# Moving expert, softmax and scan-state work between engines in a one-core AdaLN block

## The chip, the core and the metric

The kernel runs on one core of a Trainium2 chip, in fp32. The metric is the device time of one execution in microseconds (us). The engines are called by the profile's names: PE is TensorE, DVE is VectorE, ACT is ScalarE, POOL is GpSimd, SP is SyncE; PEld is the load of weights into TensorE.

## What is computed

The input x is [8 sequences, 512 steps, 128 features]. Six modulation rows per sequence (sa, ca, ga, sb, cb, gb) are made from c. Then come a recurrent attention part and a mixture of 8 experts, each behind a layernorm with modulation. Cut to what matters:

```python
h = layernorm(x) * (1 + ca) + sa
# attention part: 8 heads, state of 16, so 128 softmaxes of 17 per token
hr = rmsnorm(h) * norm_w
v = hr @ W_v.T                                  # [B, T, 8, 16]
gates = softmax((hr @ W_a.T).reshape(B, T, 8, 16, 17))
a0, A = gates[..., 0], gates[..., 1:]
state[t] = einsum('bhij,bhj->bhi', A[t], state[t-1]) + a0[t] * v[t]   # scan over 512 steps
x = x + ga * (h + state.reshape(B, T, 128) @ W_out.T)
# experts: top 4 of 8, softmax over the chosen
h = layernorm(x) * (1 + cb) + sb
combine = softmax of the 4 largest of (h @ router.T + bias), 0 elsewhere
gate, up = split(h @ gate_up.T + bias)          # 256 each, per expert
gate = minimum(gate, 7); up = clip(up, -7, 7)
act = (up + 1) * gate * sigmoid(1.702 * gate)
y = sum over experts of combine * (act @ down.T + down_bias)
x = x + gb * y
```

## The kernel before

The 4096 tokens are cut into 32 tiles of 128 tokens: 16 time steps of all 8 sequences. Four tiles make a superchunk of 512 tokens; there are 8. Up to the scan a tile has its tokens on the partitions; the scan has 64 partitions, one for each pair of head and sequence; the experts have features on the partitions and 512 tokens along the line.

The work consists of these parts, written as Python generators:

- ln1 (L188): layernorm (L162 to L179, with two full-width products with modulation rows at L178 and L179) and the rms factor of a superchunk.
- gates (L203 to L248), for a tile: transpose (L209), five matmuls into PSUM chunks of 27, 27, 26, 26 and 22 softmax groups (L220), with v in the last. For each chunk DVE takes the maximum (L224) and subtracts it (L226), ACT raises it (L229). Then, over all 128 groups of 17 (2176 elements a partition), DVE sums (L234), takes the reciprocal (L235), multiplies (L238), and multiplies the a0 column by v (L241). Eight DMAs on SP's queue (L243), one for each head, turn the tile ee (tokens on partitions) into g (heads and sequences on partitions).
- scan (L250 to L262), 16 steps for a tile: a product of the 16x16 gates with the state before (L256) and a sum over 17 (L259), which writes the new state into ys in SBUF. Each step needs the one before.
- attn_out (L264 to L282): eight DMAs on SP turn ys back into yt (L269), then transpose (L273), copy (L275), the output matmul (L277), and the addition into r (L281).
- attn_post (L284 to L357), for a superchunk: residual (L287, L288), second layernorm, transposes to h2T (L293, L295), the router matmul pr (L300), ranking and softmax on small tiles (L305 to L340), which give comb, the weight of each expert for each token. Then comb is transposed (L345) and multiplied with the experts' output biases (L350); the result is where the sum y begins (L355).
- experts (L359 to L423), for two experts at a time: for each of two halves of 128 features, gate and up matmuls of 512 tokens (L365, L367); ACT adds biases (L371, L373) and takes the sigmoid (L375); DVE clips up (L382), multiplies by min(gate, 7) (L383) and by the sigmoid (L384). The down projection (L391) has act as the weights, 128 tokens at a time, so an expert takes eight matmuls of 128 columns, and its output pd has tokens on the partitions. The combination (L399) is four operations an expert, each with a weight per partition: y = pd * comb + y.
- finish (L425 to L432): product with gb (L427), residual (L428), four output DMAs on SP (L431).

The order comes from two places. In the main loop (L443 to L462), beside the 16 scan steps of tile c, the kernel writes out the other parts: attn_out of tile c-1, ln1, the gates of tile c+2, attn_post of the superchunk before (beside the first tile of a superchunk), and its experts, two beside each of the four tiles, then finish. After each scan step two pieces of this list are taken:

```python
        for _ in scan(c):
            next(other, None)
            next(other, None)
        run(other)
```

The Tile framework then orders the instructions of each engine when the kernel is built, by its own planning, and puts in the waits on semaphores; at run time every engine works through its own list in that order. In the built kernel all eight experts of a superchunk lie in one stretch. Pools limit how far parts run ahead: two buffers of ee, three of g and ys, and in PSUM two banks for gate chunks, three for gate and up, one for pd, and two for all the small ones (misc).

Of the kernel before, what the change touches and what calls it, by code (L numbers as in the profile page):

```python
# [9 lines left out]
F32 = mybir.dt.float32  # L10
# [9 lines left out]
SIG_MAX = 1.0 / (1.0 + math.exp(-ALPHA * LIMIT))  # L20
# [8 lines left out]
def adaln_block_kernel(  # L29
    ctx: ExitStack,  # L30
    tc: tile.TileContext,
    x: bass.AP,        # [B, T, D]
    norm_w: bass.AP,   # [D, 1]
    wa_t: bass.AP,     # [D, H*M*(M+1)]
    wv_t: bass.AP,     # [D, D]
    wo_t: bass.AP,     # [D, D]
    rw_t: bass.AP,     # [D, E]
    r_bias: bass.AP,   # [1, E]
    gu_t: bass.AP,     # [D, E*2I]
    gu_bias: bass.AP,  # [128, E*4]  # L40
    dn_t: bass.AP,     # [E, I, D]
    dn_bias: bass.AP,  # [E, D]
    c_in: bass.AP,     # [B, D]
    w_mod: bass.AP,    # [D, 6*D]
    out: bass.AP,      # [B, T, D]
# [4 lines left out]
    J = M + 1               # softmax width  # L50
    NG = H * M              # softmax groups per token
    TT = P // B             # time steps in a tile of 128 tokens
    NT = T // TT            # tiles
    KT = 4                  # tiles in a superchunk
# [5 lines left out]
    # (first softmax group, groups) of each PSUM bank; v goes into the last bank  # L60
# [12 lines left out]
    ps_misc = ctx.enter_context(tc.tile_pool(name="ps_misc", bufs=2, space=PS))  # L73
# [45 lines left out]
    # lower[e, f] = 1 where f < e: among equal logits the lower index goes first  # L119
# [6 lines left out]
    # up's bias with the 1 of (up + 1)  # L126
# [54 lines left out]
    # the parts below are generators: they yield where other work may come between  # L181
    h_tiles = {}      # superchunk -> (h, rms factor)
    g_tiles = {}      # tile -> gates for the scan
    y_tiles = {}      # tile -> scan states
    r_tiles = {}      # superchunk -> h + attention
    f_tiles = {}      # superchunk -> what the experts need
# [16 lines left out]
    def gates(c):  # L203
# [12 lines left out]
        for g0, n in CHUNKS:  # L216
            last = g0 + n == NG
            w = n * J + (D if last else 0)
            pg = ps_gate.tile([P, 512], F32, tag="pg", name=f"pg{c}_{g0}")
            nc.tensor.matmul(  # L220
                pg[:, :w], hnT, wav[:, g0 * J : g0 * J + w], start=True, stop=True
            )
            pg3 = pg[:, : n * J].rearrange("p (g j) -> p g j", j=J)
            nc.vector.tensor_reduce(mx[:, g0 : g0 + n], pg3, AX.X, ALU.max)  # L224
            e3 = ee[:, g0 : g0 + n, :]
            nc.vector.tensor_tensor(  # L226
                e3, pg3, mx[:, g0 : g0 + n].unsqueeze(2).to_broadcast([P, n, J]), ALU.subtract
            )
            nc.scalar.activation(e3, e3, AF.Exp)  # L229
            if last:  # L230
                nc.scalar.copy(v, pg[:, n * J : w])
            yield
        z = tile_p.tile([P, NG], F32, tag="z", name=f"z{c}")
# [4 lines left out]
        nc.vector.tensor_tensor(  # L238
            ee, ee, z.unsqueeze(2).to_broadcast([P, NG, J]), ALU.mult
        )  # L240
        nc.vector.tensor_tensor(ee[:, :, 0], ee[:, :, 0], v, ALU.mult)  # L241
# [8 lines left out]
    def scan(c):  # L250
        g = g_tiles.pop(c)
        ys = scan_p.tile([H * B, TT, M], F32, tag="ys", name=f"ys{c}")
        prev = state0 if c == 0 else y_tiles[c - 1][:, TT - 1, :]
# [8 lines left out]
        y_tiles[c] = ys  # L262
# [21 lines left out]
    def attn_post(s):  # L284
        r = r_tiles.pop(s)
        x1 = sc_p.tile([P, KT, D], F32, tag="x1", name=f"x1_{s}")
        nc.vector.tensor_tensor(r, r, mod_row(2), ALU.mult)  # L287
        nc.vector.tensor_tensor(x1, r, x_sb[:, s * KT : (s + 1) * KT, :], ALU.add)  # L288
        h2 = sc_p.tile([P, KT, D], F32, tag="h2", name=f"h2_{s}")
# [7 lines left out]
        # router: top 4 of 8, softmax over the chosen  # L297
# [44 lines left out]
        # the experts' output biases, weighted  # L342
# [5 lines left out]
        pb = misc_psum(f"pb{s}")  # L348
        for k in range(KT):
            nc.tensor.matmul(  # L350
                pb[:, k * D : (k + 1) * D], cT[:, k * P : (k + 1) * P], dnb_sb,
                start=True, stop=True,
            )
        y = sc_p.tile([P, KT, D], F32, tag="y", name=f"y{s}")
        nc.scalar.copy(y.rearrange("p k d -> p (k d)"), pb)  # L355
        f_tiles[s] = (x1, h2T, comb, y)
        yield  # L357

    def experts(s, es):  # L359
        x1, h2T, comb, y = f_tiles[s]  # L360
        acts = {}

        def front(e, ic):
# [6 lines left out]
            gt = ffn_p.tile([P, NW], F32, tag="gate", name=f"gate{s}_{e}_{ic}")  # L370
            nc.scalar.activation(gt, pgt, AF.Identity, bias=gub_sb[:, e, ic : ic + 1])  # L371
            up = ffn_p.tile([P, NW], F32, tag="up", name=f"up{s}_{e}_{ic}")
            nc.scalar.activation(up, pup, AF.Identity, bias=ub1_sb[:, e, ic : ic + 1])  # L373
            sg = ffn_p.tile([P, NW], F32, tag="sg", name=f"sg{s}_{e}_{ic}")
            nc.scalar.activation(sg, gt, AF.Sigmoid, scale=ALPHA)  # L375
            return gt, up, sg

        def back(e, ic, gt, up, sg):
            if ic == 0:
                acts[e] = ffn_p.tile([P, IC, NW], F32, tag="act", name=f"act{s}_{e}", bufs=2)  # L380
            # clip(up, -7, 7) + 1, min(gate, 7), sigmoid(1.702 min(gate, 7))
            nc.vector.tensor_scalar(up, up, 1.0 - LIMIT, 1.0 + LIMIT, ALU.max, ALU.min)  # L382
            nc.vector.scalar_tensor_tensor(up, gt, LIMIT, up, ALU.min, ALU.mult)  # L383
            nc.vector.scalar_tensor_tensor(acts[e][:, ic, :], sg, SIG_MAX, up, ALU.min, ALU.mult)  # L384

        def down(e):
            act = acts.pop(e)
            pd = ps_dn.tile([P, KT, D], F32, tag="pd", name=f"pd{s}_{e}")
            for k in range(KT):
                for ic in range(IC):  # L390
                    nc.tensor.matmul(  # L391
                        pd[:, k, :], act[:, ic, k * P : (k + 1) * P], dn_sb[:, e * IC + ic, :],
                        start=(ic == 0), stop=(ic == IC - 1),
                    )
            return pd

        def combine(e, pd):
            for k in range(KT):
                nc.vector.scalar_tensor_tensor(  # L399
                    y[:, k, :], pd[:, k, :], comb[:, k, e : e + 1], y[:, k, :], ALU.mult, ALU.add  # L400
                )
# [23 lines left out]
    def finish(s):  # L425
        x1, _, _, y = f_tiles.pop(s)
        nc.vector.tensor_tensor(y, y, mod_row(5), ALU.mult)  # L427
        nc.vector.tensor_tensor(y, y, x1, ALU.add)  # L428
        for k in range(KT):
            c = s * KT + k  # L430
            nc.sync.dma_start(out[:, c * TT : (c + 1) * TT, :], y[:, k, :])  # L431
        yield  # L432
# [5 lines left out]
    # ---- the pipeline: beside the scan of tile c run the gates of tile c + 2,  # L438
    # the output of tile c - 1 and a part of the experts of the superchunk before
# [67 lines left out]
```

## Time and profile before

Three runs: 1391.12 us median (1390.35 to 1391.66). The profiled execution has a span of 1390.6 us.

| what | us |
|---|---|
| median of the runs | 1391.12 |
| span of the profiled execution, its own time | 1390.6 |
| DVE busy | 1151.2 |
| PE busy | 675.7 |
| PE weight loads | 348.3 |
| ACT busy | 462.8 |
| POOL busy | 1.1 |
| DVE, clip of up (L382), 128 instructions of 423 ns | 54.2 |
| DVE, reciprocal of the sums (L235), 32 of 938 ns | 30.0 |
| DVE, a0 times v (L241), 32 of 374 ns | 12.0 |
| ACT, sigmoid (L375), 128 of 629 ns | 80.5 |
| ACT, exp of chunks (L229), 160 of 564 ns on average | 89.1 |

Busy times of the engines overlap, so they don't add up to the span. In a line of the profile's groups, the source line and engine come first, then the operation, the tile written and the tiles read with their shapes, the number of instructions, the busy time in us with the mean of one in ns, and last the time for which the engine was idle just before, with what ended most of that. The slices cut the span into 40 parts of 34.8 us; each digit is a busy share in tenths. The chain of work is followed back from the last instruction, from each step to what released it.

### The profile page before, as it was taken

How to read it: one execution, taken by the hardware profiler on the slowest of the kernel's cores; microseconds unless marked ns; L12 is line 12 of the kernel's file. 1: busy time of each engine (PE TensorE's matmuls, PEld its weight loads, DVE VectorE, ACT ScalarE, POOL GpSimd, SP SyncE). 2: the span in 40 equal slices, each digit the busy share in tenths (PEclk: the TensorE clock that was granted, in tenths of full speed). 3: DMA queues.
4: the chain of work that ended last, by engine and by line, in shares of the span. 5: the costliest groups of instructions: out<-in, count | busy, mean ns of one | idle time of the engine just before them, and what ended most of it. 6: DMA issues, size and time to landing. Idle time of an engine off the chain costs nothing.

```text
span 1390.6 us, 9491 instructions
## 1 busy us (share of the span) xinstructions
PE 675.7 (49%) x2181; PEld 348.3 (25%) x2181; DVE 1151.2 (83%) x2533; ACT 462.8 (33%) x850; POOL 1.1 (0%) x10
## 2 busy tenths in 40 slices
PE   1415049531594237830496315942369414771077
PEld 0101015310262014510153102620135201440044
DVE  3889699996999799996989969897898978888366
ACT  2401037320382115610373203821146102541054
POOL 0000000000000000000000000000000000000000
PEclk9755568865697667965688656976569756795579
DMA  6251514024330325005140242303241041501200
GB/s 199 32 60 14 60 21 49 1 32 45 36 31 10 44 25 65 2 11 63 20 51 0 30 48 33 34 10 38 31 50 17 10 54 20 61 1 21 24 0 8
DMA packets 80248, 47.39 MB, mean 34 GB/s; under 512 B 38064, under 2 KB 79296, under 8 KB 79936
## 3 DMA queue, kind: packets, MB, share of 16 engines
q1 hardware_dynamic: 78640, 42.03, 25.8%
q10 hardware_dynamic: 1552, 4.75, 1.0%
q14 instruction: 38, 0.31, 0.1%
q8 instruction: 18, 0.29, 0.1%
HBM read 6.91 MB, written 2.10 MB: 6 GB/s over the span
## 4 chain that ended last, share of the span: by engine, by line
DVE 40%; PE 32%; DMA 21%; issue 2%; SPq 2%; ACT 2%; DVEq 0%; ACTq 0%
DMA g<-ee 15%; PE pgt L365 9%; PE pd L391 8%; DVE g L256 8%; PE pup L367 8%; DVE ys L259 7%; DVE mx L224 5%; DVE z L234 5%; DMA yt<-ys 4%; PE pg L220 4%; DVE ee L226 4%; DVE ee L238 3%; SPq L243 2%; DVE z L235 2%; DMA x_sb<-in_x_dram 1%
## 5 line engine op out<-in xcount | busy, mean ns | idle before, releaser
L256 DVE TENSOR_TENSOR g<-g,ys 64x256 f32<-64x256 f32 x511 | 211.2, 413 | 107.0 <-DMA g<-ee 60.1
L220 PE MATMUL pg<-wav,hnT 128*128 128x459 f32 (+2 forms) x320 | 221.6, 815 | 133.5 <-DVE ee L226 108.7
L259 DVE TENSOR_REDUCE ys<-g 64x16 f32<-64x272 f32 x512 | 217.1, 424 | 11.3
L273 PE MATMUL py<-ident,yt 128*128 128x128 f32 x32 | 13.7, 427 | 436.5 <-DMA yt<-ys 435.8
L275 ACT COPY ytT<-py 128x128 f32<-128x128 f32 x32 | 8.5, 266 | 513.1 <-PE py L273 513.1
L391 PE MATMUL pd<-dn_sb,act 128*128 128x128 f32 x1024 | 146.6, 291 | 29.8 <-DVE act L384 16.2
L391 PEld LDWEIGHTS pd<-dn_sb,act 128*128 128x128 f32 x1024 | 136.2, 201 | 91.3 <-DVE act L384 36.6
L229 ACT ACTIVATE ee<-ee 128x459 f32<-128x459 f32 (+2 forms) x160 | 89.1, 564 | 201.4 <-DVE ee L226 179.6
L365 PE MATMUL pgt<-h2T,gu_sb 128*128 128x512 f32 x256 | 145.9, 654 | 0.0
L367 PE MATMUL pup<-h2T,gu_sb 128*128 128x512 f32 x256 | 138.8, 625 | 0.0
L220 PEld LDWEIGHTS pg<-wav,hnT 128*128 128x128 f32 x320 | 68.9, 254 | 257.2 <-issue 163.1
L273 PEld LDWEIGHTS py<-ident,yt 128*128 128x128 f32 x32 | 6.2, 193 | 461.3 <-issue 302.2
L224 DVE TENSOR_REDUCE mx<-pg 128x27 f32<-128x459 f32 (+2 forms) x160 | 95.1, 594 | 13.5 <-PE pg L220 12.8
L373 ACT ACTIVATE up<-pup,ub_sb 128x512 f32<-128x512 f32 x128 | 86.8, 678 | 40.8 <-PE pup L367 40.8
L371 ACT ACTIVATE gate<-pgt,gub_sb 128x512 f32<-128x512 f32 x128 | 87.6, 684 | 24.7 <-PE pgt L365 24.2
L226 DVE TENSOR_TENSOR ee<-pg,mx 128x459 f32<-128x459 f32 (+2 forms) x160 | 95.2, 595 | 0.0
L384 DVE SCALAR_TENSOR_TENSOR act<-sg,up 128x512 f32<-128x512 f32 x128 | 88.1, 688 | 7.4 <-ACT sg L375 3.4
L383 DVE SCALAR_TENSOR_TENSOR up<-gate,up 128x512 f32<-128x512 f32 x128 | 88.0, 688 | 2.9
L399 DVE SCALAR_TENSOR_TENSOR y<-pd,comb,y 128x128 f32<-128x128 f32 x256 | 74.9, 342 | 14.2 <-PE pd L391 13.9
L375 ACT ACTIVATE sg<-gate 128x512 f32<-128x512 f32 x128 | 80.5, 629 | 2.5
L234 DVE TENSOR_REDUCE z<-ee 128x128 f32<-128x2176 f32 x32 | 76.8, 2400 | 0.5 <-ACT ee L229 0.5
L238 DVE TENSOR_TENSOR ee<-ee,z 128x2176 f32<-128x2176 f32 x32 | 76.9, 2404 | 0.0
(89 smaller groups left out, 599.1 us busy)
## 6 DMA issues: line engine op xcount, KB each, us to landing
g<-ee SPq DMA_DIRECT2D x256, 136.0 KB
yt<-ys SPq DMA_DIRECT2D x256, 8.0 KB
x_sb<-in_x_dram SPq DMA_DIRECT2D x32, 64.0 KB
gu_sb<-in_gu_t_dram ACTq DMA_DIRECT2D x1, 2048.0 KB
out_dram<-y SPq DMA_DIRECT2D x32, 64.0 KB
wav<-in_wa_t_dram ACTq DMA_DIRECT2D x1, 1088.0 KB
wmod_sb<-in_w_mod_dram ACTq DMA_DIRECT2D x1, 384.0 KB
wo_sb<-in_wo_t_dram SPq DMA_DIRECT2D x1, 64.0 KB
```

Source lines behind the costliest of these rows:

```text
L220: nc.tensor.matmul(pg[:, :w], hnT, wav[:, g0 * J : g0 * J + w], start=True, stop=True)
L224: nc.vector.tensor_reduce(mx[:, g0 : g0 + n], pg3, AX.X, ALU.max)
L226: nc.vector.tensor_tensor(e3, pg3, mx[:, g0 : g0 + n].unsqueeze(2).to_broadcast([P, n, J]), ALU.subtract)
L229: nc.scalar.activation(e3, e3, AF.Exp)
L234: nc.vector.tensor_reduce(z, ee, AX.X, ALU.add)
L238: nc.vector.tensor_tensor(ee, ee, z.unsqueeze(2).to_broadcast([P, NG, J]), ALU.mult)
L256: nc.vector.tensor_tensor(a, a, prev.unsqueeze(1).to_broadcast([H * B, M, M]), ALU.mult)
L259: nc.vector.tensor_reduce(ys[:, t, :], g[:, t, :, :], AX.X, ALU.add)
L365: nc.tensor.matmul(pgt, gu_sb[:, e, ic * P : (ic + 1) * P], h2T, start=True, stop=True)
L367: nc.tensor.matmul(pup, gu_sb[:, e, I + ic * P : I + (ic + 1) * P], h2T, start=True, stop=True)
L384: nc.vector.scalar_tensor_tensor(acts[e][:, ic, :], sg, SIG_MAX, up, ALU.min, ALU.mult)
L391: nc.tensor.matmul(pd[:, k, :], act[:, ic, k * P : (k + 1) * P], dn_sb[:, e * IC + ic, :], start=(ic == 0), stop=(ic == IC - 1),)
```

## The change

- Gates: ACT copies the five PSUM chunks to ee. One DVE maximum over all 128 groups follows, then POOL subtracts it (2176 elements), one ACT exp covers the whole tile, DVE sums and takes the reciprocal, and POOL does the product with it and the product of the a0 column with v. The DMAs of g follow as before.
- Scan: the states are written into one PSUM bank yp with two halves, one for each parity of the tile, and the next step reads them from there. ACT copies a tile's states into ys in SBUF when its 16 steps are done; the yt DMAs read that.
- Experts: silu(1.702 gate + bias) on ACT takes the place of the identity and the sigmoid; the factor 1/1.702 goes into the weights of the combination. POOL clips up. One DVE operation, min with silu's value at 7 and product, takes the place of two. The down projection has the projection as weights and 512 tokens moving, so an expert takes two matmuls of 512 columns, and pd has features on the partitions.
- Combination: since tokens now lie along the line, weights must stand on all partitions. comb's transpose, over 1.702, is written to DRAM (cD) and read back with every partition getting all 8 x 512 values (wB, 2048 KB), both on ACT's DMA queue. DVE multiplies pd by wB's part, POOL adds to the sum yT.
- finish: eight matmuls transpose yT with the identity and add the weighted output biases, both into one bank; DVE reads that.
- Pools: misc has one PSUM bank instead of two (the states take the other), up five buffers, h2, y, yT and wB one each; x1 uses r's memory.

The core of the diff:

```diff
@@ gates
-            nc.vector.tensor_reduce(mx[:, g0 : g0 + n], pg3, AX.X, ALU.max)
-            e3 = ee[:, g0 : g0 + n, :]
-            nc.vector.tensor_tensor(
-                e3, pg3, mx[:, g0 : g0 + n].unsqueeze(2).to_broadcast([P, n, J]), ALU.subtract
-            )
-            nc.scalar.activation(e3, e3, AF.Exp)
+            nc.scalar.copy(ee[:, g0 : g0 + n, :], pg3)
...
+        nc.vector.tensor_reduce(mx, ee, AX.X, ALU.max)
+        yield
+        nc.gpsimd.tensor_tensor(
+            ee, ee, mx.unsqueeze(2).to_broadcast([P, NG, J]), ALU.subtract
+        )
+        yield
+        nc.scalar.activation(ee, ee, AF.Exp)
+        yield
...
-        nc.vector.tensor_tensor(
+        nc.gpsimd.tensor_tensor(
             ee, ee, z.unsqueeze(2).to_broadcast([P, NG, J]), ALU.mult
         )
-        nc.vector.tensor_tensor(ee[:, :, 0], ee[:, :, 0], v, ALU.mult)
+        nc.gpsimd.tensor_tensor(ee[:, :, 0], ee[:, :, 0], v, ALU.mult)
@@ scan
-        ys = scan_p.tile([H * B, TT, M], F32, tag="ys", name=f"ys{c}")
-        prev = state0 if c == 0 else y_tiles[c - 1][:, TT - 1, :]
+        ys = yp[:, c % 2, :, :]
+        prev = state0 if c == 0 else yp[:, (c - 1) % 2, TT - 1, :]
...
-        y_tiles[c] = ys
+        y_tiles[c] = scan_p.tile([H * B, TT, M], F32, tag="ys", name=f"ys{c}")
+        nc.scalar.copy(y_tiles[c], ys)
@@ attn_post
-        pb = misc_psum(f"pb{s}")
-        for k in range(KT):
-            nc.tensor.matmul(
-                pb[:, k * D : (k + 1) * D], cT[:, k * P : (k + 1) * P], dnb_sb,
-                start=True, stop=True,
-            )
-        y = sc_p.tile([P, KT, D], F32, tag="y", name=f"y{s}")
-        nc.scalar.copy(y.rearrange("p k d -> p (k d)"), pb)
-        f_tiles[s] = (x1, h2T, comb, y)
+        cA = ffn_p.tile([P, NW], F32, tag="w", name=f"cA{s}", bufs=2)
+        nc.scalar.mul(cA[:E, :], pc[:E, :], 1.0 / ALPHA)
+        cD = dram.tile([E, NW], F32, tag="cD", name=f"cD{s}")
+        nc.scalar.dma_start(cD, cA[:E, :])
+        wB = sc_p.tile([P, E, NW], F32, tag="wB", name=f"wB{s}", bufs=1)
+        nc.scalar.dma_start(wB, cD.rearrange("e n -> (e n)").unsqueeze(0).to_broadcast([P, E * NW]))
+        f_tiles[s] = (x1, h2T, cT, wB)
@@ experts
-            gt = ffn_p.tile([P, NW], F32, tag="gate", name=f"gate{s}_{e}_{ic}")
-            nc.scalar.activation(gt, pgt, AF.Identity, bias=gub_sb[:, e, ic : ic + 1])
-            up = ffn_p.tile([P, NW], F32, tag="up", name=f"up{s}_{e}_{ic}")
+            sg = ffn_p.tile([P, NW], F32, tag="sg", name=f"sg{s}_{e}_{ic}")
+            nc.scalar.activation(sg, pgt, AF.Silu, bias=gb_sb[:, e, ic : ic + 1], scale=ALPHA)
+            up = ffn_p.tile([P, NW], F32, tag="up", name=f"up{s}_{e}_{ic}", bufs=5)
             nc.scalar.activation(up, pup, AF.Identity, bias=ub1_sb[:, e, ic : ic + 1])
-            sg = ffn_p.tile([P, NW], F32, tag="sg", name=f"sg{s}_{e}_{ic}")
-            nc.scalar.activation(sg, gt, AF.Sigmoid, scale=ALPHA)
+            nc.gpsimd.tensor_scalar(up, up, 1.0 + LIMIT, 1.0 - LIMIT, ALU.min, ALU.max)
...
-            nc.vector.tensor_scalar(up, up, 1.0 - LIMIT, 1.0 + LIMIT, ALU.max, ALU.min)
-            nc.vector.scalar_tensor_tensor(up, gt, LIMIT, up, ALU.min, ALU.mult)
-            nc.vector.scalar_tensor_tensor(acts[e][:, ic, :], sg, SIG_MAX, up, ALU.min, ALU.mult)
+            nc.vector.scalar_tensor_tensor(up, sg, SILU_MAX, up, ALU.min, ALU.mult)
...
-            for k in range(KT):
-                for ic in range(IC):
-                    nc.tensor.matmul(
-                        pd[:, k, :], act[:, ic, k * P : (k + 1) * P], dn_sb[:, e * IC + ic, :],
-                        start=(ic == 0), stop=(ic == IC - 1),
-                    )
+            for ic in range(IC):
+                nc.tensor.matmul(
+                    pd, dn_sb[:, e * IC + ic, :], act[ic],
+                    start=(ic == 0), stop=(ic == IC - 1),
+                )
...
-            for k in range(KT):
-                nc.vector.scalar_tensor_tensor(
-                    y[:, k, :], pd[:, k, :], comb[:, k, e : e + 1], y[:, k, :], ALU.mult, ALU.add
-                )
+            if e == 0:
+                yT_tiles[s] = sc_p.tile([P, NW], F32, tag="yT", name=f"yT{s}", bufs=1)
+                nc.vector.tensor_tensor(yT_tiles[s], pd, wB[:, e, :], ALU.mult)
+                return
+            w = ffn_p.tile([P, NW], F32, tag="w", name=f"w{s}_{e}", bufs=2)
+            nc.vector.tensor_tensor(w, pd, wB[:, e, :], ALU.mult)
+            nc.gpsimd.tensor_tensor(yT_tiles[s], yT_tiles[s], w, ALU.add)
@@ finish
+        pb = misc_psum(f"pb{s}")
+        for k in range(KT):
+            blk = slice(k * P, (k + 1) * P)
+            nc.tensor.matmul(pb[:, blk], yT[:, blk], ident, start=True, stop=False)
+            nc.tensor.matmul(pb[:, blk], cT[:, blk], dnb_sb, start=False, stop=True)
```

## The prediction

> **What bounds the kernel now.** I read the engine totals first, then the slices, the chain of work that ended last, the groups, and last one superchunk by windows.
>
> ```profile
> PE 675.7 (49%) x2181; PEld 348.3 (25%) x2181; DVE 1151.2 (83%) x2533; ACT 462.8 (33%) x850; POOL 1.1 (0%) x10
> DVE  3889699996999799996989969897898978888366
> POOL 0000000000000000000000000000000000000000
> DVE 40%; PE 32%; DMA 21%; issue 2%; SPq 2%; ACT 2%; DVEq 0%; ACTq 0%
> L256 DVE TENSOR_TENSOR g<-g,ys 64x256 f32<-64x256 f32 x511 | 211.2, 413 | 107.0 <-DMA g<-ee 60.1
> L259 DVE TENSOR_REDUCE ys<-g 64x16 f32<-64x272 f32 x512 | 217.1, 424 | 11.3
> L384 DVE SCALAR_TENSOR_TENSOR act<-sg,up 128x512 f32<-128x512 f32 x128 | 88.1, 688 | 7.4 <-ACT sg L375 3.4
> L383 DVE SCALAR_TENSOR_TENSOR up<-gate,up 128x512 f32<-128x512 f32 x128 | 88.0, 688 | 2.9
> L399 DVE SCALAR_TENSOR_TENSOR y<-pd,comb,y 128x128 f32<-128x128 f32 x256 | 74.9, 342 | 14.2 <-PE pd L391 13.9
> L234 DVE TENSOR_REDUCE z<-ee 128x128 f32<-128x2176 f32 x32 | 76.8, 2400 | 0.5 <-ACT ee L229 0.5
> L238 DVE TENSOR_TENSOR ee<-ee,z 128x2176 f32<-128x2176 f32 x32 | 76.9, 2404 | 0.0
> ```
>
> VectorE is 83% busy and GpSimd idle, which looks like one full engine. But the chain gives VectorE only 40% of the span, TensorE 32% and DMA 21%: the work passes from one to the next. The fifth superchunk shows it; in the chain the columns are start, length, what:
>
> ```profile
> 628.92 15.72 DMA g<-ee
> 644.65 17.74 DMA g<-ee
> 662.41 1.96 DMA yt<-ys
> 699.14 1.88 PE pr L300 x8
> ```
>
> ```profile
> 599.70:624.00 24.30, 9.48 (x17) 3.56 (x17) 22.51 (x43) 5.89 (x12) 0.00 (x0) 0.64 0.06 14
> 624.00:644.80 20.80, 3.57 (x4) 0.86 (x4) 12.48 (x22) 2.18 (x5) 0.00 (x0) 0.58 0.53 61
> 644.80:662.50 17.70, 0.00 (x0) 0.00 (x0) 13.47 (x32) 0.00 (x0) 0.00 (x0) 0.50 0.57 58
> 662.50:699.10 36.60, 18.38 (x32) 6.79 (x32) 35.27 (x69) 11.04 (x22) 0.00 (x0) 0.64 0.20 23
> 699.10:749.40 50.30, 47.08 (x198) 28.46 (x198) 44.81 (x113) 36.01 (x63) 0.00 (x0) 0.93 0.30 31
> 749.40:763.80 14.40, 5.74 (x22) 3.96 (x22) 12.95 (x34) 0.92 (x3) 0.00 (x0) 0.78 0.00 0
> ```
>
> The columns are: length, busy time of PE, PEld, DVE, ACT, POOL, then clock, DMA share, GB/s. In order: gates beside a scan (VectorE full), the first tile's g transfer (20.8 us), the second's (17.7, a scan alone beside it), gates of two more tiles and attn_post (VectorE full), the eight experts (TensorE 47 of 50.3, VectorE close behind), the rest of the last scan. A period is 164 us: the router matmul starts at 210.85, then every 160 to 164 us, the last 140.2 later, and 59.5 us before the end.
>
> [...]with lines of 459 and 374 elements from PSUM (0.62, 0.53 us) and 2176 from SBUF (2.40) the fixed part is about 0.14 us for both[...] g, 1088 KB in small pieces, takes 17.7 here[...].
>
> **Part by part.** *VectorE's load.* The max goes from 95.1 to 32 x 2.40 = 76.8; the subtraction (95.2), L238 (76.9), the a0 product (12.0), L383 (88.0) and the clip (54.2) leave; the combination goes from 74.9 to 64 x 0.68 = 43.5. Together 376 us off 1151. It is no sum for the span, since only the full stretches use it.
>
> *Gate chain.* Before, each chunk is reduced, subtracted and raised while the next is multiplied, and the first g leaves 24.3 us after the scan before it ended. In the built kernel's order ScalarE first copies the old scan's states out of PSUM and so waits for that scan's end, with all that follows queued behind: yt's transfer and its two matmuls (4.5 from transfer to hnT, as from 662.41 in the chain; the one bank left in ps_misc makes each transpose wait until the last is read, VectorE's L296 among the readers, about 0.7), then five matmuls at the lower clock with a copy each (about 1.2): ee is full at 11.4. Then in series max 2.4 (among scan steps, to 14.1), subtraction on GpSimd, exp 2.0 (0.25 for 128 elements at L231, 0.56 for 512 at L355, so 0.82 ns an element), sum, a step and reciprocal 3.9, product and a0 on GpSimd (5.3 with 0.5 for 128 elements). [...] g leaves at 14.1 + 4.8 + 2.1 + 4.0 + 5.4 = 30.4, +6.1. The second tile's chain ends under the first transfer (46 against 50.8), so its 17.8 us stay as they are.
>
> *Stretch before the router.* VectorE had 35.3 us of 36.6 here. Without the subtraction, product and a0 (about 12 us for two tiles) and with the max serial it should take 24.6: [...] one yt transfer is queued on SP behind the 16 g issues (about +3). The router starts at 93.2 after the scan's end instead of 99.4: a gain of 6.
>
> *Scan.* [...] The step (0.91 us) I take as unchanged[...]. ScalarE's copy to SBUF (0.3) stands ahead of each yt transfer: +0.7 with its wait, 32 times but on the path only at D and the end.
>
> *Experts.* TensorE's two passes over 512 tokens (2 x 0.86) replace eight of 128 (1.78): nothing. Silu saves an ScalarE pass; VectorE does 2 x 0.69 + 0.68 = 2.1 us an expert where it did 5.0[...]. So these edits gain nothing while TensorE is full: at most the 50.3 - 47.1 = 3 us. But the first product with wB waits. After comb (about 107, some 14 us after the router as before, GpSimd's product of the next gates ahead of the first clip) come the transposes, cA, a write to DRAM (2 us, for which ScalarE stands at the next issue, the rest of expert 1 and all later fronts behind it), and a 2 MB read back on ScalarE's queue with one buffer, whose last reader, the superchunk before, is long done: [...]5 at the 409 GB/s that gu_sb reached at best[...]. I take 9 to 10: wB at 120 to 123. VectorE stands in order before it: the next experts' products queue behind, TensorE fills its buffers (three gate/up banks, one pd) and stops, about 10 to 13 us. From there some 35 us of TensorE work, plus GpSimd's subtraction and product for the next tiles ahead of clips (5): the last act at about 162 instead of 149.7. The last scan had five steps under the experts' tail; its steps are now queued behind that tail: 15.3 instead of 14.4. Period 178 instead of 164: +14 (between +2 and +30).
>
> *finish.* Eight small matmuls and an addition that reads PSUM take the place of the bias that began y: +1 to 2, beside the scan's tail, shown only at the end.
>
> *Sum.* Prologue: no other work covers the first four chains, and each is longer by two GpSimd passes (9.6), max and exp (4.5), less L238 (2.4): 4 x 11.7 = 47, of which the shorter stretch before the router gives back 12: +35. (In a period it is only 6.1, since there VectorE was shared with a scan and the second tile's chunks.) Six periods +84. Last period: its last gates have no tiles behind them and pass under wB's wait: 124 where it had 140.2, -16. Epilogue: wB's wait and finish, less VectorE's smaller load, +4. That is +107, and on the profiled 1390.6 it gives 1498; the runs' median is 0.5 above the span, so the same.
>
> **Rivals.** *A, VectorE is the bound and the freed time pays.* For it: 83% busy, two stretches full. Price: with GpSimd at 2.4 and no lock, g leaves 4.8 earlier, the router at about 84; if wB lands within 8 us of comb, VectorE loses 4, the last act is at 138, the period 153: six x -11, prologue +16, last -20, epilogue -2 = -72, 1319 (1300 to 1385). It decides by the g issue: under 26 us after a scan's end, with wB in before the second expert's product. Against it: four serial steps where chunks overlapped. *B, mild.* GpSimd costs its 4.8, but nothing is locked and wB comes in 7: period 167; 30 + 18 - 16 = +32, 1423 (1400 to 1455). *C, wB slow.* If the broadcast shares the DMA engines with g (20 us and more)[...] the period is 192: 35 + 168 - 10 + 8 = +201, 1592 (1550 to 1640). *That GpSimd doesn't get the work* is excluded: the order of the built kernel has it there.
>
> **From cases to numbers.** Mine (1455 to 1550) 0.46, B 0.20, A 0.17, C 0.15, no change 0.02. A difference under 0.2% could not be told from none. The range leaves out A but for its edge (0.15) and C's end (0.05): 1380 to 1590.
>
> **What would show it.** Right: GpSimd about 450 to 500 us busy, its 2176-element products 4.5 to 5 us; g issue about 30 us after a scan's end; VectorE near 775 us busy; a wait of the first product for wB of about 10 us a superchunk; the clock falling there. Wrong: a wB that lands before the first pd; scan steps other than 0.91 us; a GpSimd product below 3 us or above 7; scan steps slipping in among the experts.

## The result, and the profile after

The changed kernel takes 1587.12 us (median of four runs, 1584.29 to 1588.2) against 1391.39 for the kernel before: a ratio of 1.14, with a 95% interval of 1.1384 to 1.1416. The profiled execution's span is 1586.2. The forecast was slower, 1498, with 1380 to 1590 as its range.

These are lines of the page of the changed kernel: engine totals, the slices of VectorE and GpSimd, the shares of the chain that ended last by engine and by line, and five groups.

```profile
PE 697.1 (44%) x1477; PEld 302.5 (19%) x1477; DVE 886.9 (56%) x1734; ACT 490.8 (31%) x811; POOL 432.3 (27%) x290
DVE  3485575373754738447482564826556373753732
POOL 0422302414015131251321521224312414025013
DVE 34%; DMA 24%; PE 20%; POOL 8%; issue 5%; ACT 4%; SPq 4%; POOLq 0%; ACTq 0%; DVEq 0%
DMA g<-ee 10%; PE pg L231 9%; DVE yp L273 8%; DVE g L270 8%; DMA cD<-cA 5%; PE pd L401 4%; DMA wB<-cD 4%; POOL ee L252 4%; DMA yt<-ys 4%; DVE mx L239 4%; DVE z L248 3%; SPq L257 3%; DVE h L181 2%; PE pup L381 2%; DVE le L327 2%
L241 POOL TENSOR_TENSOR ee<-ee,mx 128x2176 f32<-128x2176 f32 x32 | 125.1, 3910 | 601.5 <-DVE mx L239 559.2
L270 DVE TENSOR_TENSOR g<-g,yp 64x256 f32<-64x256 f32 x511 | 209.1, 409 | 129.2 <-DMA g<-ee 80.1
L273 DVE TENSOR_REDUCE yp<-g 64x16 f32<-64x272 f32 x512 | 222.1, 434 | 14.6
L394 DVE SCALAR_TENSOR_TENSOR up<-sg,up 128x512 f32<-128x512 f32 x128 | 87.9, 688 | 218.2 <-POOL up L389 218.2
L389 POOL TENSOR_SCALAR up<-up 128x512 f32<-128x512 f32 x128 | 81.8, 639 | 220.7 <-ACT up L387 215.4
```

VectorE is no longer full anywhere: 56% busy where it had 83%, and no engine took its place. The chain has new links: GpSimd 8%, and two transfers that did not exist, cD<-cA with 5% and wB<-cD with 4% of the span. L394 is named as waiting 218.2 us for GpSimd, but GpSimd's clip waited as long for ScalarE. The engine that a wait names is only its last link; what held the first link is read from the chain.

The chain of the sixth superchunk (start, length, what):

```profile
1217.94 11.62 DMA cD<-cA
1229.57 8.72 DMA wB<-cD
1238.32 0.70 DVE yT L410
```

A write of 16 KB takes 11.6 us, then the 2 MB read takes 8.7, and only then comes the first product with a weight. TensorE is busy for 8.8 of these 20.4 us. In SyncE's timeline, what was issued just before the write:

```profile
1212.53 17.64 SPq L257 DMA_DIRECT2D g<-ee  x8
```

A g transfer starts 5.4 us before the write of the weights is issued, and the DMA engines move 59 GB/s on average from the issue of the write to its landing. The last of g's packets ends at 1228.9, the first packet of the write runs at 1227.5, and the write lands at 1229.6. The eighth of g's DMAs is issued only then, which makes the line of SyncE 17.6 us long.

What else is new shows in two timelines, VectorE's and GpSimd's, at the router:

```profile
1207.16 3.88 DVE L327 TENSOR_TENSOR le<-lg,lmx 128x32 f32<-128x32 f32 x1
```

```profile
1207.02 3.98 POOL L252 TENSOR_TENSOR ee<-ee,z 128x2176 f32<-128x2176 f32 x1 [8.56 <-DVE lmx L325]
```

L327 works on 32 elements and took 0.188 us in the kernel before (L312 there). Here it started 0.14 us after GpSimd's product and ended with it. It did so in seven superchunks of eight; in the eighth, with no GpSimd product beside it, it took 0.18.

### The profile page after: what moved, and what is told of

The parts are those of the page before. It is cut to its first block, busy times and chain, and to the rows that moved or that the text cites. A ratio compares the mean times of both kernels' runs of the same rounds, so it can differ in the third digit from the quotient of the medians.

```text
span 1586.2 us, 7381 instructions
## 1 busy us (share of the span) xinstructions
PE 697.1 (44%) x1477; PEld 302.5 (19%) x1477; DVE 886.9 (56%) x1734; ACT 490.8 (31%) x811; POOL 432.3 (27%) x290
## 4 chain that ended last, share of the span: by engine, by line
DVE 34%; DMA 24%; PE 20%; POOL 8%; issue 5%; ACT 4%; SPq 4%; POOLq 0%; ACTq 0%; DVEq 0%
DMA g<-ee 10%; PE pg L231 9%; DVE yp L273 8%; DVE g L270 8%; DMA cD<-cA 5%; PE pd L401 4%; DMA wB<-cD 4%; POOL ee L252 4%; DMA yt<-ys 4%; DVE mx L239 4%; DVE z L248 3%; SPq L257 3%; DVE h L181 2%; PE pup L381 2%; DVE le L327 2%
## 5 line engine op out<-in xcount | busy, mean ns | idle before, releaser
L241 POOL TENSOR_TENSOR ee<-ee,mx 128x2176 f32<-128x2176 f32 x32 | 125.1, 3910 | 601.5 <-DVE mx L239 559.2
L270 DVE TENSOR_TENSOR g<-g,yp 64x256 f32<-64x256 f32 x511 | 209.1, 409 | 129.2 <-DMA g<-ee 80.1
L273 DVE TENSOR_REDUCE yp<-g 64x16 f32<-64x272 f32 x512 | 222.1, 434 | 14.6
L231 PE MATMUL pg<-wav,hnT 128*128 128x459 f32 (+2 forms) x320 | 194.7, 764 | 78.0 <-ACT ee L235 50.3
L394 DVE SCALAR_TENSOR_TENSOR up<-sg,up 128x512 f32<-128x512 f32 x128 | 87.9, 688 | 218.2 <-POOL up L389 218.2
L288 PE MATMUL py<-ident,yt 128*128 128x128 f32 x32 | 11.9, 371 | 425.9 <-DMA yt<-ys 425.9
L401 PE MATMUL pd<-up,dn_sb 128*128 128x512 f32 x256 | 152.1, 695 | 105.2 <-DVE up L394 62.4
L252 POOL TENSOR_TENSOR ee<-ee,z 128x2176 f32<-128x2176 f32 x32 | 127.4, 3982 | 178.4 <-DVE z L249 119.3
L389 POOL TENSOR_SCALAR up<-up 128x512 f32<-128x512 f32 x128 | 81.8, 639 | 220.7 <-ACT up L387 215.4
L235 ACT COPY ee<-pg 128x459 f32<-128x459 f32 (+2 forms) x160 | 81.6, 520 | 166.3 <-PE pg L231 129.7
L277 ACT COPY ys<-yp 64x256 f32<-64x256 f32 x32 | 11.7, 364 | 358.0 <-DVE yp L273 328.3
L385 ACT ACTIVATE sg<-pgt,gb_sb 128x512 f32<-128x512 f32 x128 | 88.0, 688 | 99.7 <-PE pgt L379 99.0
L414 POOL TENSOR_TENSOR yT<-yT,w 128x512 f32<-128x512 f32 x56 | 77.4, 1382 | 137.8 <-DVE w L413 136.9
L245 ACT ACTIVATE ee<-ee 128x2176 f32<-128x2176 f32 x32 | 64.5, 2017 | 117.9 <-POOL ee L241 117.9
L288 PEld LDWEIGHTS py<-ident,yt 128*128 128x128 f32 x32 | 5.3, 165 | 446.4 <-issue 423.1
```

The source lines that it names most:

```text
L231: nc.tensor.matmul(pg[:, :w], hnT, wav[:, g0 * J : g0 * J + w], start=True, stop=True)
L241: nc.gpsimd.tensor_tensor(ee, ee, mx.unsqueeze(2).to_broadcast([P, NG, J]), ALU.subtract)
L252: nc.gpsimd.tensor_tensor(ee, ee, z.unsqueeze(2).to_broadcast([P, NG, J]), ALU.mult)
L270: nc.vector.tensor_tensor(a, a, prev.unsqueeze(1).to_broadcast([H * B, M, M]), ALU.mult)
L273: nc.vector.tensor_reduce(ys[:, t, :], g[:, t, :, :], AX.X, ALU.add)
L385: nc.scalar.activation(sg, pgt, AF.Silu, bias=gb_sb[:, e, ic : ic + 1], scale=ALPHA)
```

## The experiments

All times are medians beside runs of the kernel before on the same chip (1390 to 1392 us), four runs each, and 20 of the order alone on the kernel before. With E for the experts' part, S for the softmax part and C for the scan states in PSUM:

| kernel | us | ratio to before | 95% interval |
|---|---|---|---|
| before | 1391 | 1 | |
| E alone | 1437.9 | 1.0341 | 1.0299 to 1.0384 |
| S alone | 1501.6 | 1.0802 | 1.0773 to 1.0831 |
| C alone | 1437.6 | 1.0349 | 1.0312 to 1.0386 |
| E + C | 1469.0 | 1.0564 | 1.0547 to 1.058 |
| S + C | 1464.3 | 1.0523 | 1.0505 to 1.054 |
| E + S + C, the change | 1587.1 | 1.14 | 1.1384 to 1.1416 |
| change, wB constant | 1454.5 | 1.0474 | 1.0448 to 1.05 |
| change, wB by matmul | 1586.6 | 1.1382 | 1.1324 to 1.1441 |
| change, attn_post first | 1456.3 | 1.0469 | 1.0452 to 1.0485 |
| before, one misc bank | 1417.1 | 1.0184 | 1.0157 to 1.0212 |
| before, silu, clip on GpSimd | 1381.5 | 0.9925 | 0.991 to 0.994 |
| before, attn_post first | 1394.5 | 1.0023 | 1.0016 to 1.003 |
| before, both of these | 1372.3 | 0.9855 | 0.9838 to 0.9872 |

### The experts' part alone

The gates, the scan and the pools of PSUM stay as in the kernel before; the rest is as changed.

> The kernel before with the experts' part of the change alone (silu, one product, clip and sum on GpSimd, turned down projection, weights read back from DRAM); softmax and scan as before. Theory W (the loss of the change is the wait for wB, since the 16 KB write of the weights queues behind a g transfer in the DMA engines): nearly the whole loss of the periods is here, 18 to 24 us in each of six and some in the last, none in the prologue: 1500 to 1545. Rival S (the loss is the softmax chain in series on GpSimd): 1370 to 1410.

Measured: 1437.9, +47. Both theories missed. The weights make the same trip through DRAM, but in ScalarE's timeline cD is issued at 565.39 and wB at 567.67: the write took 2.3 us (1.8 to 3.3 over the eight superchunks), where it takes 9.8 to 12.0 in the first seven of the changed kernel. The first product comes 21 to 25 us after the router instead of 14, and the last act at 56 to 59 instead of 50, 6 to 9 us later in each period. So the trip alone is not the whole loss; something makes it slow when the softmax part is there too.

What differs is not when g's transfer starts: here its first DMA leaves SyncE 7.9 to 9.0 us before the write in the first seven superchunks, in the changed kernel 5.1 to 6.7. But a g transfer is eight DMAs, and SyncE's waits (total, times, longest) show those that are held back; the first two lines are of this kernel, the third is of the changed one:

```profile
SPq L252 <- DMA wB<-cD: 63.1, 7, 10.2
SPq L252 <- DMA cD<-cA: 59.0, 7, 9.2
SPq L257 <- DMA cD<-cA: 79.9, 7, 12.7
```

Here two of the eight leave before the write, and the third waits until the write has landed; the later ones wait for the read too. The code doesn't ask for these waits; the trace shows only that the landing ends them. So the DMA engines are almost idle while the write runs (a share of 0.04 from 565.4 to 567.7). In the changed kernel seven leave before it and only the eighth waits.

### The softmax part alone

```diff
-        nc.vector.tensor_tensor(
+        nc.gpsimd.tensor_tensor(
             ee, ee, z.unsqueeze(2).to_broadcast([P, NG, J]), ALU.mult
         )
```

with the whole of the gates as changed, and nothing else.

> The kernel before with the softmax part alone (one maximum, subtraction and product on GpSimd); experts and scan as before. Theory W: the prologue pays 33 us, the periods gain nothing or lose little (g leaves 10 us later, the stretch before the router is 15 us shorter, scan steps with two SBUF inputs may be held off by GpSimd): 1400 to 1440. Rival S: 1500 and more.

Measured: 1501.6, +111. The prologue paid 37 us (first router at 248.2 where it was 210.9), near the 33 of theory W; the rest came in the periods, which W had at little or nothing, though it named the cause. They are 137 to 141 us and 219 us in turn. One line of its page, and then one from each of the timelines of VectorE and GpSimd, show where:

```profile
L259 DVE TENSOR_TENSOR g<-g,ys 64x256 f32<-64x256 f32 x511 | 291.5, 570 | 116.3 <-DMA g<-ee 77.1
```

```profile
853.19 4.12 DVE L259 TENSOR_TENSOR g<-g,ys 64x256 f32<-64x256 f32 x1
```

```profile
853.15 3.89 POOL L230 TENSOR_TENSOR ee<-ee,mx 128x2176 f32<-128x2176 f32 x1 [34.75 <-DVE mx L228]
```

A scan step's product, 0.413 us on average before, takes 4.12 when it starts just after a GpSimd operation, and ends 0.2 us after it. Over the kernel these products grew by 80 us.

### Scan states in PSUM alone, and one bank alone

The first has L264 to L277 of the changed kernel; the second is one number of the kernel before:

```diff
-    ps_misc = ctx.enter_context(tc.tile_pool(name="ps_misc", bufs=2, space=PS))
+    ps_misc = ctx.enter_context(tc.tile_pool(name="ps_misc", bufs=1, space=PS))
```

> The kernel before with the scan states in PSUM alone (ScalarE copies them to SBUF once a tile, one bank fewer for small tiles). Both theories: a step stays at 0.91 us; the copy ahead of the yt transfers and the single bank cost up to 2 us at a tile where that is on the path: 1391 to 1420.

> The kernel before with one PSUM bank for the small tiles instead of two, nothing else. Theory B (the 47 us of the scan states in PSUM are the bank that they took away): 1425 to 1445. Rival C (they are ScalarE's copy of the states ahead of the yt transfers and of the gates): 1388 to 1400.

Measured: 1437.6 (+47) and 1417.1 (+26). The step is the same length (with the states in PSUM the product takes 408 ns and the sum 432, where the kernel before has 413 and 424), so the first expectation was wrong about the cost, not about the step. Neither theory of the second fits alone: the bank is about half, and by difference ScalarE's copy with its wait is some 21 us; the copy was not tried alone. The view of waits of the one-bank kernel, then of the kernel before (who waits for whom, total, times, longest), names what the bank holds up:

```profile
ACT hnT L211 <- PE ph L209: 162.8, 25, 17.0
```

```profile
ACT hnT L211 <- PE ph L209: 31.0, 30, 1.2
```

With one bank the transpose of the next tile's input stands behind the output of the tile before, which waits for the yt transfer: in the same view of the one-bank kernel the transposes (L209) wait 130.7 us for the addition into r (L281), which frees the bank.

### Softmax and scan states together

```diff
-        ys = scan_p.tile([H * B, TT, M], F32, tag="ys", name=f"ys{c}")
+        ys = yp[:, c % 2, :, :]
```

and the softmax part; experts as before.

> The kernel before with the softmax part and the scan states in PSUM; experts as before. Theory L (in the softmax part alone GpSimd holds off scan steps, whose product has two SBUF inputs; with the state in PSUM it can't): the 80 us by which the product's busy time grew mostly go, the single small bank costs its 26: 1430 to 1475. Rival N (the holding off lay beside other waits): the costs add, 1502 + 47 = 1549: 1520 to 1560.

Measured: 1464.3, inside theory L's range and far from the sum of the two parts. Two groups of its page:

```profile
L266 DVE TENSOR_REDUCE yp<-g 64x16 f32<-64x272 f32 x512 | 222.2, 434 | 15.0
L263 DVE TENSOR_TENSOR g<-g,yp 64x256 f32<-64x256 f32 x511 | 209.1, 409 | 96.5 <-DMA g<-ee 45.9 <-DMA yt<-ys 31.4 <-ACT ys L270 5.2
```

The product is back at 409 ns with the same GpSimd work beside it: the state in PSUM is what frees it. So C, which costs 47 by itself, takes 37 off when S is there.

### Without the trip of the weights

```diff
-        cA = ffn_p.tile([P, NW], F32, tag="w", name=f"cA{s}", bufs=2)
-        nc.scalar.mul(cA[:E, :], pc[:E, :], 1.0 / ALPHA)
-        cD = dram.tile([E, NW], F32, tag="cD", name=f"cD{s}")
-        nc.scalar.dma_start(cD, cA[:E, :])
-        wB = sc_p.tile([P, E, NW], F32, tag="wB", name=f"wB{s}", bufs=1)
-        nc.scalar.dma_start(wB, cD.rearrange("e n -> (e n)").unsqueeze(0).to_broadcast([P, E * NW]))
+        wB = wB_c
```

> The changed kernel with wB a constant that is written once: the write to DRAM and the 2 MB read are left out, and with them the routing weights in the sum. Theory W: the 22.6 us between the weights and the first product go to 1 or 2; TensorE is full in their place, so 16 to 20 us a period come back: 1440 to 1475. Rival G (GpSimd's clips and sums set the experts' pace, the wait for wB only hides it): 1540 and more.

Measured: 1454.5, as theory W expected. Between the first and the seventh router a period is 171.8 us where the changed kernel has 191.1, 19.3 us less, and its write and read together take about 20. (The edit also frees the products from waiting for comb, but the first of them still starts after comb is ready, by 0.8 to 4.7 us in these superchunks.) Rival G falls by its number: GpSimd does the same clips, sums and softmax here, 436 us of them.

A part of what G says remains, though. From the first product with a weight to the last act (the operand of the down projection) this kernel takes 46 to 48 us, where the kernel before, E alone and E + C take 34 to 37. In those three no gates fall into that stretch; here a whole tile's do, with two GpSimd operations of 3.9 us ahead of the clips. ScalarE also loads its function table more often: 79 loads of 1.28 us here and in the changed kernel, where 30 of them stand at the silu (L385) and 22 at the exp of the gates (L245), 54 before (16 at the sigmoid, 17 at the exp), 52 to 58 with one or two of E, S and C. What each of these costs was not tried.

### The trip kept, the order changed

```diff
+        if s > 0 and k == 0:
+            beside.append(attn_post(s - 1))
         if c + 2 < NT:
             beside.append(gates(c + 2))
         if s > 0:
-            if k == 0:
-                beside.append(attn_post(s - 1))
             beside.append(experts(s - 1, range(k * E // KT, (k + 1) * E // KT)))
```

> The changed kernel with attn_post written ahead of the gates beside the first tile of a superchunk (two lines change places), so that the router's weights are made, and written to DRAM, before that tile's g transfer starts. Theory W with the collision: the write takes 2 to 3 us instead of 11.6, 9 us a period and some more as the weights come earlier: 1470 to 1525. Rival Q: the write is as slow as before and the time stays over 1560.

Measured: 1456.3, below the range that was expected, and as much as the constant wB gave back. It also holds both cases side by side. In the second, fourth and sixth superchunk the router still comes after a g issue; in the first, third, fifth and seventh it doesn't. SyncE's queue and the chain for the second, then ScalarE's queue for the third, where the last g issue was at 544.00:

```profile
384.38 7.60 SPq L257 DMA_DIRECT2D g<-ee  x8
```

```profile
398.58 6.57 DMA cD<-cA
405.17 7.13 DMA wB<-cD
```

```profile
591.75 0.29 ACTq L367 DMA_DIRECT2D cD<-cA  x1
594.27 0.33 ACTq L369 DMA_DIRECT2D wB<-cD  x1
```

With g in flight the write takes 6.6 us, until 2.3 us after the last of g's packets (402.9); without it, 2.5. Over the seven superchunks it is 6.2 to 6.9 and 1.6 to 2.6. That is the collision, within one kernel. The seven writes take 29 us together instead of 80, so their length is 51 of the 131 us; the rest comes with the order, by which the gates themselves lie elsewhere, and this run does not part it. Nor can its uneven periods (148 to 156 and 188 to 192 us in turn) be put down to the write: S + C, without one, has 139 to 141 and 206.

### The gates back on VectorE

The changed kernel with the gates of before.

> The changed kernel with the gates of before (softmax on VectorE in chunks); experts and scan states as changed. Theory W with the collision (the 16 KB write takes 11.6 us only because GpSimd's slower softmax lets a g transfer start just before it): the write lands in 2 to 3 us as in the experts' part alone, and the two parts' costs add, 1391 + 47 + 47 = 1485: 1465 to 1505. Rival Q (a write of the weights after the scan states went to PSUM is slow anyhow): the write takes 10 us and more and the time is 1530 or above.

Measured: 1469.0, within the range. The write takes 1.8 to 3.1 us in all eight superchunks, with scan states in PSUM and wB as changed: rival Q falls. SyncE again holds g back: two of its eight DMAs leave before the write, and the rest wait for the write and the read (91.5 and 66.6 us). Without S, the change loses 78 us instead of 196.

### Weights by matmul

```diff
-        cD = dram.tile([E, NW], F32, tag="cD", name=f"cD{s}")
-        nc.scalar.dma_start(cD, cA[:E, :])
         wB = sc_p.tile([P, E, NW], F32, tag="wB", name=f"wB{s}", bufs=1)
-        nc.scalar.dma_start(wB, cD.rearrange("e n -> (e n)").unsqueeze(0).to_broadcast([P, E * NW]))
+        for e in range(E):
+            pw = misc_psum(f"pw{s}_{e}")
+            nc.tensor.matmul(pw, ident[:E, e : e + 1].to_broadcast([E, P]), cA[:E, :], start=True, stop=True)
+            nc.scalar.copy(wB[:, e, :], pw)
```

> The changed kernel with the weights spread over the partitions by eight matmuls of 512 columns with a column of the identity as weights and eight ScalarE copies, in place of the write to DRAM and the 2 MB read. Theory W: the first product starts about 3 us after the weights instead of 22.6, TensorE gets 8 x 0.86 = 7 us more a superchunk and ScalarE 8 x 0.59; with 1454 for the kernel with a constant wB as the floor: 1475 to 1520. Rival: one small PSUM bank, used in turn by matmul and copy, makes it as slow as the DRAM trip: 1550 and more.

Measured: 1586.6 (1570.9 to 1590.6; its profiled execution has 1569.2, so the profile explains what lies 1% below the median). Theory W missed. The number is the rival's, the reason is not. The first product does start 4 to 7 us after the weights, but in the window from the weights to the last act of the sixth superchunk TensorE is busy for 51.6 of 60.3 us (length; busy PE, PEld, DVE, ACT, POOL; clock, DMA share, GB/s):

```profile
1188.70:1249.00 60.30, 51.62 (x113) 18.70 (x112) 25.55 (x31) 31.12 (x49) 25.78 (x23) 0.97 0.22 25
```

The eight matmuls of the weights follow each other at 2.1 us, with one other matmul between each two and no pause that the profile shows, so the bank, which goes to and fro between matmul and copy, does not stop TensorE; TensorE has 8 x 1.05 = 8.4 us more to do, in front of the experts' own work. Why the last act comes 12 us later than with a constant wB (73.9 against 61.6 after the router, in the second superchunk), and not 8.4, stays open.

### What is worth keeping

Two edits from this, put on the kernel before. First, silu with one product and the clip on GpSimd, with the down projection, the combination, the softmax and the scan left alone:

```diff
+            nc.scalar.activation(sg, pgt, AF.Silu, bias=gb_sb[:, e, ic : ic + 1], scale=ALPHA)
...
+            nc.gpsimd.tensor_scalar(up, up, 1.0 + LIMIT, 1.0 - LIMIT, ALU.min, ALU.max)
...
+            nc.vector.scalar_tensor_tensor(acts[e][:, ic, :], sg, SILU_MAX, up, ALU.min, ALU.mult)
```

> The kernel before with silu on ScalarE, one product on VectorE and the clip on GpSimd, 1/1.702 in the weights; the down projection, the combination, the softmax and the scan as before, so no weights go through DRAM. Theory P (TensorE sets the experts' pace, VectorE's freed 142 us lie beside it): at most 3 to 8 us a superchunk, 1345 to 1385. Rival V (VectorE was the bound there and in what follows): 1290 to 1340. Rival G (GpSimd's clip in the chain[...]): 1395 and more.

> The kernel before with attn_post written ahead of the gates beside the first tile of a superchunk, nothing else. TensorE starts the experts about 13 us earlier, and VectorE gets a tile's gates (12 us) beside them, where it had 45 of 50 us: most is given back, 1345 to 1395. If the order of the stretch didn't matter: 1391.

> Both of the last two edits: silu with the clip on GpSimd, and attn_post ahead of the gates. Theory P: the VectorE time that silu frees beside the experts (about 18 us a superchunk) now holds the gates that were moved there, so the 12 us a period are kept: 1270 to 1335. Rival: a g transfer that now starts later comes out as a wait of the next scan, and it is no better than the better of the two alone.

Measured: 1381.5, 1394.5 and 1372.3. Silu alone gives 0.75%: VectorE's freed time (busy 1027 us instead of 1151) lay beside TensorE, as theory P had it, and the 10 us are near the low end of what it allowed. The order alone costs 0.23%: the first router comes 9 us earlier, but the experts' last act comes 59.8 us after the router instead of 50.3, with a tile's gates now beside them on VectorE and 72 table loads on ScalarE instead of 54, and the period stays 164 us. Which of the two holds the experts up was not tried. Together they give 1.45%, the fastest of all these kernels and faster than both that were compared. The last expectation (1270 to 1335) is missed all the same: the experts still end later, 54.9 us after the router, and a period is 161 us, not 151. Its waits on VectorE:

```profile
DVE act L385 <- POOL up L379: 100.8, 90, 4.3
DVE g L259 <- DMA g<-ee: 64.9, 8, 8.4
DVE g L259 <- DMA yt<-ys: 36.7, 8, 16.9
```

The two waits of the scan for its transfers are those of the kernel before (68.3 and 34.9), and none of the edits touches them. That they bound the period is a guess; no run takes them away.

## Why the prediction held, and where it was short

The direction was right, and both of its causes are in the traces: the gate chain in series, and VectorE and TensorE standing until wB lands. The size was not: the forecast rise of 107 us is 55% of the measured 196. The range held by 3 us at its upper end, and in part by luck: the case that the prediction favoured (1455 to 1550) was missed, and the time lies where rival C had it (1550 to 1640), of which the range took in only the lower part. By the terms of its sum, read off the router's starts (243.83, 437.58, ... 1390.34, 1521.08) and the span:

| term | before | predicted | measured |
|---|---|---|---|
| to the first router | 210.9 | 246 | 243.8 |
| a period, mean of six | 163.3 | 177 to 178 | 191.1 |
| last period | 140.2 | 124 | 130.7 |
| after the last router | 59.5 | 63.5 | 65.1 |

The prologue, the epilogue and the sign of the last period held. The error is some 14 us in each of the six periods, 82 us of the 89. Within the period that ends with the scan at 1296.1, after the scan's end at 1108.6:

| event | before | predicted | measured |
|---|---|---|---|
| first g issued | 24.3 | 30.4 | 34.1 |
| router | 99.4 | 93.2 | 94.1 |
| weights comb ready | 106 | 107 | 107.1 |
| wB landed | none | 120 to 123 | 129.7 |
| last act begun | 149.7 | 162 | 170.4 |
| last scan ended | 164.1 | 178 | 187.5 |

**The step that failed is the term for wB**: "a write to DRAM (2 us ...)" and "I take 9 to 10". The read was right (7.2 to 9.7 us measured), the write was not: 2 us is what it takes alone (1.8 in the last superchunk), and 9.8 to 12.0 with a g transfer ahead of it, 9.4 us a period more than was reckoned. The 2 us were the author's estimate; no run had shown such a write. The prediction had named the sharing with g, but only for the read, where no trace shows its 20 us, and had put it into rival C, whose period of 192 us and 1592 us are what was measured. The missed question was how much of the g transfer would be in the DMA queues when the write is issued: seven of its eight DMAs in the changed kernel, two in E alone and E + C, where SyncE holds the rest back behind the write. That is most of the reason why E costs 47 us alone and 123 on top of S + C: a period is 6.8 us longer with E alone, 9.9 with S + C and 27.8 with all three, 11 more than the sum, and the write is 9 longer than in E alone.

The table above shows the shortest of the six periods (187.5 us). A second term of the sum was too small in the five before it: "some 35 us of TensorE work", plus 5 for GpSimd, from wB's landing to the last act. Measured from the first product it is 41.3 us in the sixth superchunk and 46.1 to 47.1 in the first five. There all of a tile's gate matmuls come after the wait for wB, and only four of the 16 acts come before it; in the sixth it is six.

Smaller terms:

- *g issue*: 3.7 us later than worked out, though GpSimd's operation was 3.9 us, not 4.8. The 4.8 us, which the prediction's prologue and rival B take too, were not shown: GpSimd is busy for 1.1 us in the trace of before. ee was full 14.1 us after the scan's end instead of 11.4. Then, in VectorE's order, the first operation of finish (L448) stands ahead of the next tile's sum; it waited 5.1 us for the matmuls of pb, and the sum started 3 us after its exp was done. The prediction had put finish beside the scan's tail, at nothing: that cover was not there.
- *The weights*: ready when predicted, for another reason than given. It said 14 us after the router "as before"; before, they were ready after 6.6, and the 12.4 to 12.8 now are GpSimd's hold on L327 (3.7) and the next tile's sum and reciprocal (3.3) ahead of it.
- *GpSimd beside VectorE*: predicted at 4.7 us once a period, for the layernorm's two products; no trace of before shows such a hold (rivals A and B call it a lock). The runs do, elsewhere: L327 took 3.88 us instead of 0.188, the scan's product in the softmax kernel 4.12 instead of 0.413, each started within 0.2 us after a GpSimd operation of 3.9 to 4.0 us and ended with it or up to 0.2 us later; with the state in PSUM the product keeps to 409 ns on average. The layernorm's products (L185, L186) took 0.69 us at most, but none of the 32 started beside a GpSimd operation. What was held in their place is eight of the 64 L181, a tensor_scalar (3.9 us, where the median is 0.33), and L327, by 3.7 us in seven superchunks.
- *VectorE's load*: 887, not 775. The 376 us were taken as sums of groups from a total in which overlapping instructions count once. The groups of before sum to 1251, so 875 was due in such a sum; the groups of the changed kernel come to 933, and the time for which L181 and L327 were held is 54 of the 58 in between.
- *Scan in PSUM*: the step was right at 0.91 us (0.92 measured, from one product's start to the next, in the median); the single bank, taken at 0.7 us a gate chain, is 26 us by itself.

Of the figures that were to show it right, the clock came as said: 0.73 granted between the weights and the first product of the sixth superchunk, against 0.93 in the experts' stretch of the kernel before. The others were off: GpSimd busy 432 us (450 to 500), its large products 3.9 to 4.0 (4.5 to 5), the g issue 34 us after a scan's end (30), VectorE 887 (775), and VectorE idle for wB 6 us a superchunk (10).

Rival A (freed VectorE time pays) had its deciding point at a g issue under 26 us; it came at 34. Its core is refuted more sharply by the silu kernel: VectorE busy for 124 us less, 10 us less time. Rival B needed wB within 7 us.

## To carry to other kernels

Work that leaves a full engine is worth only the stretches in which that engine ended last; here 83% busy was 40% of the chain. Before putting a small transfer on a path, look at what the DMA queues carry at the moment of its issue in the changed order, not at its own size: 16 KB cost 12 us behind seven of g's DMAs of 136 KB each, and 2 to 3 where most of these were issued after it. When work moves to GpSimd, see which VectorE operations take longer beside it, and change those together with the move, or not at all. Here it was the scan's product with both inputs in SBUF (4.12 us beside a GpSimd operation of 3.89), and no longer with the state in PSUM (409 ns): C lost 47 us alone and won 37 beside S.

## What the runs showed of the hardware that was not expected

- A DRAM write of 16 KB on ScalarE's queue took 1.8 to 3.3 us with the DMA engines idle or nearly so, and 9.8 to 12.0 behind seven of g's eight DMAs from SyncE's queue. What grew is the time before its first packet: 0.8 us after the issue in the last superchunk, 6.7 to 9.8 in the first seven, in which it landed no later than 1.5 us after the last packet of g. The queues are different (q10 and q1 on the page), so it isn't order within a queue. What makes it wait wasn't tried.
- GpSimd's subtraction of 128x2176 with a broadcast input took 3.9 us, 1.6 times the 2.40 of VectorE's product of that size (L238 before), but its sum of two full 128x512 tiles (L414) took 1.26 to 1.29 in 42 of 56 cases, 1.9 times the 0.68 of VectorE's (L288 before), and 1.57 to 1.78 in the other 14, each beside VectorE's L394.
- Reading and writing the scan's state in PSUM made a step neither longer nor shorter: 409 and 434 ns against 413 and 424, and 0.92 us from one product's start to the next against 0.91 in the median.
